# The last layer of a four-layer network: softplus in thirds, and another order of its side work

## The chip, the cores and the metric

The kernel runs on one core of a Trainium2 chip. The metric is the device time of one launch in microseconds (us), the median of several runs. The core has five engines, each with its own queue of instructions that it takes in order: TensorE (PE; PEld is its loading of weights), VectorE (DVE), ScalarE (ACT), GpSimd (POOL) and SyncE (SP), which here issues DMA transfers. Matmul results go to PSUM, which has eight banks of 512 fp32 columns on 128 partitions; SBUF is the large on-chip memory.

## The reference: what is computed

Four layers act on x of shape (2, 192, 96, 96), each as x + f(groupnorm(x)). Layers 0 to 2 (a deformable convolution, a Laplacian with a 1x1 convolution, a WKV scan) are not touched. Layer 3 is a state-space layer over the L = 9216 positions of an image, with 384 inner channels (three groups of 128) and 16 states per channel:

```
xz = x_flat @ W_in.T;  x_in, z_gate = split(xz)
x_conv = silu(depthwise_conv4(x_in) + conv_b)
dt, B_ssm, C_ssm = split(W_x @ x_conv)
delta = softplus(W_dt @ dt + 2 * b_dt)
h = exp(delta * A) * h + (delta * x_conv) * B_ssm      # along the positions
y = (sum over states of h * C_ssm) + D * x_conv
out = W_out @ (y * silu(z_gate))
```

Softplus is computed as relu(t) + ln(1 + exp(-|t|)), with a correction for what is lost in rounding when 1 is added: ln(w) - ((w - 1) - e), where e = exp(-|t|) and w = 1 + e as rounded.

## The kernel before

**Steps and units.** `layer3` cuts each image into pieces of 511 positions and two of about half that (265 and 264): 38 steps, 34 of them full. The recurrence of a step is done in 12 units, numbered q = 0 to 11 (three channel groups by four): a unit has 128 partitions that hold 16 states of 8 channels, and four rows r of them. In the loop at the end, k counts units over all steps, s is the step and q the unit in it.

**A unit.** `steps_of(k)` (L2356) spreads delta over the partitions with one matmul per row into one of five PSUM banks (`decays`, taken in turn); `decay(k)` (L2370) makes the exponentials in place on ScalarE; `times_b(k)` (L2346) multiplies the loaded delta * x_conv, `bu`, by B on POOL; `scan(k)` (L2379) is the recurrence on VectorE, four instructions; `times_c(k)` (L2403) multiplies three rows by C on VectorE into `hc`, and `times_c_aside(k)` (L2414) the fourth on POOL into `hp`; `sum_of(k)` (L2421, L2427) adds over the states on TensorE into one bank, `acc`, which lasts four units, and `gate(k)` (L2440) multiplies a finished `acc` by the gate into `y` on VectorE. `load(k)` (L2336) fetches `bu` from DRAM, and `keep(k)` (L2386) and a copy in `load` (L2340) carry the state on.

**The order.** Within unit k the engines get: `sum_of(k-2)`, `scan(k)`, `steps_of(k+1)`, `decay(k+1)`, `times_c(k)`, `gate(k-2)` where a group ends (q = 1, 5, 9), `times_c_aside(k-1)`, `times_b(k+2)`, `load(k+3)`, `keep(k)`. It is written out by hand and kept as written on TensorE, ScalarE, VectorE and POOL (`manual_schedule`); SyncE's queue is ordered by the planner.

**The side work.** Three generators run between the units, a piece up to the next `yield` at each `go(name)`:
- `early(s + 2)`: normalises x (xt to xn, L2223, L2227), then six projections (L2242) with their copies to `xi` and `zs`, three groups of convolution matmuls (L2262) with their eviction to `us`, and two Silu (L2268, L2269). 20 pieces.
- `late(s + 1)`: x_dbl (L2278), its copy and three small transfers, three matmuls for delta (L2303) with Abs and Relu (L2307, L2308), Exp and 1 + e over all three groups (L2310, L2311), the correction on VectorE (L2313) and Ln (L2314), and three POOL operations (L2316, L2318, L2320), the last followed by four stores to DRAM (`ud`, L2322) from which `load` reads. 13 pieces.
- `output(s - 1)`: the load of `xr`, two times three matmuls (L2452), each half followed by an addition on VectorE (L2460), and the store. 4 pieces.

All matmuls of the side work share one PSUM bank, `pe` (the pool `ps` has one buffer of each name). Dictionaries `AHEAD` and `BEHIND` and lines in the loop say which unit runs which pieces: those in `AHEAD` go before `sum_of`, those in `BEHIND` one before and one after `decay` (for "out" only the one before).

The pools that matter: `s1` has one buffer of each tile, `sb` two, `s3` three, `sc` four.

Of the kernel before, what the change touches and what calls it, by code (L numbers as in the profile page):

```python
# [6 lines left out]
F32 = mybir.dt.float32  # L7
I32 = mybir.dt.int32
AF = mybir.ActivationFunctionType
ALU = mybir.AluOpType  # L10
# [8 lines left out]
P = 128  # L19
CH = 96  # L20
# [43 lines left out]
class Net:  # L64
# [2021 lines left out]
    def layer3(self, x, out, stats):  # L2086
# [3 lines left out]
        nc, tc, ins = self.nc, self.tc, self.ins  # L2090
        TM = 511
# [8 lines left out]
        with ExitStack() as ctx:  # L2100
            wp = ctx.enter_context(tc.tile_pool(name="w3", bufs=1))
            s1 = ctx.enter_context(tc.tile_pool(name="l3s", bufs=1))
            sb = ctx.enter_context(tc.tile_pool(name="l3", bufs=2))
            s3 = ctx.enter_context(tc.tile_pool(name="l3h", bufs=3))
# [19 lines left out]
            b2 = self.load("b_dt", [P, ND], pool=wp)  # L2124
# [94 lines left out]
            def early(s):  # L2219

                b, t0, T = steps[s]
                xt = sb.tile([CH, 2, TM], F32, name="xt")[:, :, :T]
                nc.sync.dma_start(out=xt, in_=halves(x[b])[:, :, t0 : t0 + T])  # L2223
                xn = s1.tile([CH, 2, TM], F32, name="xn")[:, :, :T]
                gs, gb = gns[b]
                for k in range(2):
                    nc.scalar.activation(  # L2227
                        xn[:, k], xt[:, k], AF.Identity, bias=gb[:, k : k + 1], scale=gs[:, k : k + 1]
                    )
                us = s3.tile([P, ND, TM], F32, name="us")[:, :, :T]  # L2230
                zs = s3.tile([P, ND, TM], F32, name="zs")[:, :, :T]
                xi = s1.tile([P, ND, TM + 3], F32, name="xi")[:, :, : T + 3]
                got[s] = {"us": us, "zs": zs}
                if t0 == 0:
                    nc.gpsimd.memset(tail, 0.0)
                nc.scalar.copy(xi[:, :, 0:3], tail)
                yield

                def project(at):
                    pe = bank(T)  # L2240
                    for k in range(2):
                        nc.tensor.matmul(  # L2242
                            pe, w_in[:, k, at : at + P], xn[:, k], start=k == 0, stop=k == 1
                        )
                    return pe

                for d in range(ND):
                    pe = project(d * P)
                    yield
                    nc.scalar.copy(xi[:, d, 3:], pe)  # L2250
                    if d == ND - 1:
                        nc.scalar.copy(tail, xi[:, :, T : T + 3])
                    yield
                for d in range(ND):
                    pe = project(DI + d * P)
                    yield
                    nc.scalar.copy(zs[:, d], pe)
                    yield
                for d in range(ND):
                    pe = bank(T)  # L2260
                    for j in range(4):
                        nc.tensor.matmul(  # L2262
                            pe, taps[:, d, j], xi[:, d, j : j + T], start=j == 0, stop=j == 3
                        )
                    yield
                    nc.scalar.activation(us[:, d], pe, AF.Identity, bias=cb[:, d : d + 1])
                    yield
                nc.scalar.activation(zs, zs, AF.Silu)  # L2268
                nc.scalar.activation(us, us, AF.Silu)  # L2269
                yield  # L2270

            def late(s):
                us = got[s]["us"]
                T = steps[s][2]
                xd = sb.tile([NBC + DTR, TM], F32, name="xd")[:, :T]
                pe = bank(T)
                for d in range(ND):
                    nc.tensor.matmul(  # L2278
                        pe[: NBC + DTR], wx[:, d], us[:, d], start=d == 0, stop=d == ND - 1
                    )  # L2280
                yield
                nc.scalar.copy(xd, pe[: NBC + DTR])
                br = dr.tile([NBC * TM], F32, name="br")[: NBC * T].rearrange("(n t) -> n t", t=T)
                nc.sync.dma_start(out=br, in_=xd[:NBC])
                rows = []
                for name, at in (("cs", 0), ("bs", NST)):
                    t = sb.tile([P, TM], F32, name=name)[:, :T]
                    one = br[at : at + NST]
                    nc.sync.dma_start(
                        out=t,  # L2290
                        in_=bass.AP(one.tensor, one.offset, [[T, NST], [0, 8], [1, T]]),
                    )
                    rows.append(t)
                dl = sb.tile([P, ND, TM], F32, name="dl")[:, :, :T]
                du = s1.tile([P, ND, TM], F32, name="du")[:, :, :T]
                ud = dr.tile([ND * P * TM], F32, name="ud")[: ND * P * T]
                ud = ud.rearrange("(i v e r t) -> i v e r t", i=ND, v=NV, e=8, r=4)
                got[s].update(xd=xd, cs=rows[0], bs=rows[1], dl=dl, ud=ud)
                ln = s1.tile([P, ND, TM], F32, name="ln")[:, :, :T]
                yield  # L2300
                for d in range(ND):
                    pe = bank(T)
                    nc.tensor.matmul(  # L2303
                        pe, wdt[:, d * P : (d + 1) * P], xd, start=True, stop=True
                    )
                    yield
                    nc.scalar.activation(du[:, d], pe, AF.Abs, bias=b2[:, d : d + 1])  # L2307
                    nc.scalar.activation(dl[:, d], pe, AF.Relu, bias=b2[:, d : d + 1])  # L2308
                    yield
                nc.scalar.activation(du, du, AF.Exp, scale=-1.0)  # L2310
                nc.scalar.activation(ln, du, AF.Identity, bias=1.0)  # L2311
                yield
                nc.vector.scalar_tensor_tensor(du, ln, -1.0, du, ALU.add, ALU.subtract)  # L2313
                nc.scalar.activation(ln, ln, AF.Ln)  # L2314
                yield
                nc.gpsimd.tensor_tensor(ln, ln, du, ALU.subtract)  # L2316
                yield
                nc.gpsimd.tensor_tensor(dl, dl, ln, ALU.add)  # L2318
                yield
                nc.gpsimd.tensor_tensor(du, dl, us, ALU.mult)  # L2320
                for r in range(4):
                    nc.sync.dma_start(  # L2322
                        out=ud[:, :, :, r].rearrange("i v e t -> (v e) i t"),
                        in_=du[32 * r : 32 * r + 32],
                    )
                yield
# [72 lines left out]
            def times_c(k):  # L2399
                s, q, _, _ = where(k)  # L2400
                T = steps[s][2]
                hc = sb.tile([P, 3, TM], F32, name="hc")[:, :, :T]
                nc.vector.tensor_tensor(  # L2403
                    hc,
                    got[s]["h", q][:, :3, 1:],
                    got[s]["cc"].unsqueeze(1).to_broadcast([P, 3, T]),
                    ALU.mult,
                )
                got[s]["hc", q] = hc
# [62 lines left out]
            for k in range(2):  # L2472
# [1 line left out]
            rows_c(0)  # L2474
            steps_of(0)
            decay(0)
            AHEAD = {1: "late", 7: "early", 8: "early", 9: "early"}
            BEHIND = {
                0: "late",
                1: "late",  # L2480
                2: "late",
                3: "out",
                4: "out",
                5: "early",
                6: "early",
                7: "early",
                8: "early",
                9: "early",
                10: "early",
            }  # L2490
            running = {"out": iter(()), "late": iter(()), "early": iter(())}

            def go(name):
                next(running[name], None)

            for k in range(nk):
# [5 lines left out]
                if q == 3 and s + 2 < ns:  # L2502
                    running["early"] = early(s + 2)
                if q in AHEAD:
                    go(AHEAD[q])
                    go(AHEAD[q])
                if k >= 2:
                    sum_of(k - 2)
                if q == 0 and s:
                    rows_c(s)  # L2510
                scan(k)
                if q in (4, 5):
                    go("out")
                if k + 1 < nk:
                    steps_of(k + 1)
# [4 lines left out]
                if q in BEHIND and BEHIND[q] != "out":  # L2520
                    go(BEHIND[q])
                if q == 3:
                    go("late")
                    go("early")
                times_c(k)
                if k >= 2 and (k - 2) % NV == NV - 1:
                    gate(k - 2)
                if q == 4:
                    go("late")
                if q == 11:  # L2530
                    go("early")
                if k:
                    times_c_aside(k - 1)
                if k + 2 < nk:
                    times_b(k + 2)
                if q in (5, 6, 7):
                    go("late")
                if k + 3 < nk:
                    load(k + 3)
# [100 lines left out]
```

## Time and profile before

| | us |
|---|---|
| median of 3 runs | 10381.23 (10363.35 to 10385.16) |
| the profiled execution | 10366.8 |
| its span (first to last instruction) | 10365.0 |
| VectorE busy | 8345.7 (81%) |
| TensorE busy | 9044.9 (87%) |
| POOL busy | 6997.7 (68%) |
| ScalarE busy | 6080.6 (59%) |
| 7550 to 10050 us, in layer 3: VectorE, TensorE, POOL, ScalarE busy, of 2500 | 2332.47, 2250.93, 2228.77, 1548.58 |
| the same: granted TensorE clock | 0.90 |

The profile is of one execution. A row of a timeline gives the start, the duration, the engine, the line, the operation, `output<-input` with shapes, and in brackets the idle time of the engine before it with what ended it. Where a row stands for several instructions (x4), the duration is that of all of them. A row of waits gives the total, the number of times and the longest. The granted clock is the share of full speed that TensorE's throttle allowed. Matmul ends are modelled.

### The profile page before, as it was taken

The numbers are of one execution on the slowest core, as the hardware profiler recorded it, in microseconds if no ns is written. First come the engines' busy times: TensorE is split into PE (matmuls) and PEld (weight loads), VectorE is DVE, ScalarE is ACT, GpSimd is POOL, SyncE is SP. The second block draws the span as 40 slices with busy tenths as digits, with TensorE's granted clock in tenths as the row PEclk, the third lists the DMA queues.
The fourth block names the chain that finished last, engine by engine and source line by source line (L and its number), as shares of the span: only waits on it lengthen the run. The fifth ranks groups of instructions, "written<-read, shape, count | busy, mean of one in ns | idle before, by whom it ended". The sixth has DMA issues, their size and how long they took to land. (4 is left out here: it accounts for less than half of the span.)

```text
span 10365.0 us, 222647 instructions
## 1 busy us (share of the span) xinstructions
PE 9044.9 (87%) x87686; PEld 5317.9 (51%) x87686; DVE 8345.7 (81%) x8842; ACT 6080.6 (59%) x11850; POOL 6997.7 (68%) x5645
## 2 busy tenths in 40 slices
PE   4799999999889999999776677887889989898988
PEld 3588788788767888888622222223222222222223
DVE  5788888788677777777655789884999999999999
ACT  0366666666566777777500178664666666666665
POOL 1466666766566666666501268773888998888898
PEclk8899999999999999999888798887888998989988
DMA  8455555555434555555444344434777777777776
GB/s 148 92 140 135 136 138 136 136 135 139 112 95 131 136 136 138 136 139 138 112 125 130 125 149 154 128 110 95 171 169 172 175 173 171 172 172 169 172 168 149
DMA packets 877166, 1465.19 MB, mean 141 GB/s; under 512 B 251616, under 2 KB 682276, under 8 KB 875012
## 3 DMA queue, kind: packets, MB, share of 16 engines
q1 hardware_dynamic: 663276, 1264.09, 48.7%
q0 software_dynamic: 104000, 133.19, 5.7%
q10 hardware_dynamic: 108840, 53.57, 2.1%
q8 instruction: 701, 11.49, 0.5%
q14 instruction: 349, 2.86, 0.1%
HBM read 871.06 MB, written 381.46 MB: 121 GB/s over the span
## 5 line engine op out<-in xcount | busy, mean ns | idle before, releaser
L581 DVE TENSOR_TENSOR sp<-h 128x2304 f32<-128x2304 f32 x790 | 2160.6, 2767 | 41.9 <-ACT h L560 41.9
L2346 POOL TENSOR_TENSOR bu<-bu,bs 128x2044 f32<-128x2044 f32 (+2 forms) x456 | 1970.8, 4322 | 230.9 <-DMA bu<-ud 181.8
L2379 DVE TENSOR_TENSOR_SCAN h<-da,bu 128x512 f32<-128x512 f32 (+2 forms) x1824 | 1979.8, 1146 | 102.6 <-ACT da L2370 86.3
L605 ACT COPY st<-pt 128x512 f32<-128x512 f32 (+1 forms) x2370 | 1213.5, 515 | 1094.0 <-PE pt L597 1022.7
L597 PE MATMUL pt<-ident,sp 128*128 128x128 f32 x14220 | 1677.4, 276 | 82.0 <-DVE sp L581 38.9
L603 DVE COPY st<-pt 128x512 f32<-128x512 f32 x1580 | 1062.7, 687 | 817.7 <-PE pt L597 806.0
L597 PEld LDWEIGHTS pt<-ident,sp 128*128 128x128 f32 x14220 | 1567.6, 142 | 164.6 <-issue 96.9
L551 POOL TENSOR_TENSOR h<-u,step 128x1152 f32<-128x1152 f32 (+1 forms) x474 | 1100.6, 2340 | 672.3 <-DVE u L524 479.2
L569 POOL DMA_DIRECT2D xw<-xp_d x2500 | 1389.8, 622 | 189.0 <-PE pt L648 83.7
L2370 ACT ACTIVATE da<-da,nA 128x511 f32<-128x511 f32 (+2 forms) x1824 | 1065.0, 638 | 575.1 <-PE da L2356 567.9
L648 PE MATMUL pt<-st,xw 64*32 64x288 f32 (+1 forms) x30000 | 1095.1, 370 | 144.2 <-DVE st L603 62.1
L674 ACT COPY val<-pt 128x288 f32<-128x288 f32 (+1 forms) x3000 | 957.6, 404 | 286.7 <-PE pt L648 262.4
L2356 PE MATMUL da<-dl,spread 32*128 32x511 f32 (+2 forms) x3648 | 927.3, 659 | 117.7 <-DVE h L2379 117.6
L776 PE MATMUL pf<-main,wd 126*64 126x128 f32 (+1 forms) x17064 | 985.4, 274 | 9.7 <-DMA far_m<-val 9.2
L776 PEld LDWEIGHTS pf<-main,wd 126*64 126x64 f32 x17064 | 912.9, 140 | 155.8 <-issue 150.9
L2403 DVE TENSOR_TENSOR hc<-h,cc 128x1533 f32<-128x1533 f32 (+2 forms) x456 | 755.1, 1656 | 171.3 <-PE acc L2427 169.3
L648 PEld LDWEIGHTS pt<-st,xw 64*32 64x32 f32 x30000 | 546.4, 106 | 558.4 <-ACT val L674 170.1
L797 PE MATMUL pf<-more,wl 118*64 118x144 f32 (+5 forms) x11592 | 732.7, 277 | 2.3 <-DMA more<-far_l 2.0
L797 PEld LDWEIGHTS pf<-more,wl 118*64 118x64 f32 (+1 forms) x11592 | 665.0, 137 | 69.6 <-issue 63.2
L2356 PEld LDWEIGHTS da<-dl,spread 32*128 32x128 f32 x3648 | 297.9, 195 | 708.3 <-DVE h L2379 491.0
L2414 POOL TENSOR_TENSOR hp<-h,cs 128x511 f32<-128x511 f32 (+2 forms) x456 | 555.4, 1218 | 68.4 <-DVE h L2379 39.1
L2242 PE MATMUL pe<-xn,sb_w_in 96*128 96x511 f32 (+2 forms) x912 | 507.6, 686 | 91.3 <-ACT xi L2250 41.5
(344 smaller groups left out, 13105.0 us busy)
## 6 DMA issues: line engine op xcount, KB each, us to landing
bu<-ud SPq DMA_DIRECT2D x408, 1022.0 KB
main<-val SPq DMA_DIRECT2D x2016, 91.1 KB
far_l<-val SPq DMA_DIRECT2D x288, 324.0 KB
xw<-xp_d POOLq DMA_DIRECT2D x2500, 26.0 KB
far_m<-val SPq DMA_DIRECT2D x288, 162.0 KB
half_d<-hv SPq DMA_DIRECT2D x54, 768.0 KB
hv<-half_d SPq DMA_DIRECT2D x54, 768.0 KB
more<-far_l SPq DMA_DIRECT2D x576, 60.8 KB
```

The costliest lines, as they stand in the source:

```text
L551: nc.gpsimd.tensor_tensor(hs, u[:, :, 8 * KK * l : 8 * KK * l + n].unsqueeze(3).to_broadcast([P, 2, n, WS]), con["step"].unsqueeze(1).unsq ...
L569: nc.gpsimd.dma_start(out=xw[e * WN : (e + 1) * WN, i], in_=xp_d[y : y + WS, x : x + WS, e * CM // 2 : e * CM // 2 + XW],)
L581: nc.vector.tensor_tensor(sp.rearrange("p s (y x) -> p s y x", x=WS), hy.unsqueeze(3).to_broadcast([P, n, WS, WS]), hx.unsqueeze(2).to_bro ...
L597: nc.tensor.transpose(pt[:, q], sp[:, 2 * (q0 + q) : 2 * (q0 + q) + 2].rearrange("p e w -> p (e w)"), self.ident,)
L605: nc.scalar.copy(st[:, q0 : q0 + m], pt[:, :m])
L648: nc.tensor.matmul(to, xw[e * WN : (e + 1) * WN, win, g * CG : g * CG + 32], sts[pair][e * WN : (e + 1) * WN].rearrange("p s (r c) -> p s ...
L776: nc.tensor.matmul(place(cv, m, 2 - t // 3, 2 - t % 3, None, 0), con["wd"][:, cv, t, m * CO : (m + 1) * CO], blocks(took, 1, rows), start= ...
L797: nc.tensor.matmul(place(cv, m, 2 * cv if alone else 1 - cv, 2 - t, h, 1 - alone,), con["wl"][lanes, slot, t, m * CO : (m + 1) * CO], bloc ...
L2346: nc.gpsimd.tensor_tensor(bu, bu, got[s]["bs"].unsqueeze(1).to_broadcast([P, 4, steps[s][2]]), ALU.mult)
L2356: nc.tensor.matmul(das[r][:, 1:], spread[at, v].rearrange("p n e -> p (n e)"), got[s]["dl"][at, i], start=True, stop=True, tile_position=( ...
L2370: nc.scalar.activation(da, da, AF.Exp, scale=nA[:, 4 * q + r : 4 * q + r + 1])
L2379: nc.vector.tensor_tensor_scan(h[:, r], got[s]["da", q][r], bu[:, r], 0.0, ALU.mult, ALU.add)
```

## The change

It touches `layer3` alone.

- In `late`, each third of softplus is finished by itself: Relu, then Abs in place in the `pe` bank, Exp in place there, 1 + e into `ln`, and the correction on VectorE with one operand from that bank. Before, Abs went to SBUF, and Exp, 1 + e and the correction ran over all three thirds. `late` has 15 pieces now, and Ln comes by itself after the last correction.
- `late` runs in q = 0 to 3 behind (one piece before and one after `decay`), with one more piece after `times_c` in q = 1, 2, 3 (the correction of the third) and Ln in q = 3; the POOL operations go in q = 4, 5, 6 instead of 5, 6, 7.
- `output`'s matmuls go in q = 4 and 5 instead of 3 and 4, its additions in 5 and 6 instead of 4 and 5.
- `early`'s pieces go in q = 6 to 11 instead of 5 to 11 (its first in q = 3 as before); q = 10 gets four.
- `hc` has three buffers instead of two, and `xt` one instead of two.

```diff
-                xt = sb.tile([CH, 2, TM], F32, name="xt")[:, :, :T]
+                xt = s1.tile([CH, 2, TM], F32, name="xt")[:, :, :T]
...
-                    nc.scalar.activation(du[:, d], pe, AF.Abs, bias=b2[:, d : d + 1])
                     nc.scalar.activation(dl[:, d], pe, AF.Relu, bias=b2[:, d : d + 1])
+                    nc.scalar.activation(pe, pe, AF.Abs, bias=b2[:, d : d + 1])
+                    nc.scalar.activation(pe, pe, AF.Exp, scale=-1.0)
+                    nc.scalar.activation(ln[:, d], pe, AF.Identity, bias=1.0)
                     yield
-                nc.scalar.activation(du, du, AF.Exp, scale=-1.0)
-                nc.scalar.activation(ln, du, AF.Identity, bias=1.0)
-                yield
-                nc.vector.scalar_tensor_tensor(du, ln, -1.0, du, ALU.add, ALU.subtract)
+                    nc.vector.scalar_tensor_tensor(
+                        du[:, d], ln[:, d], -1.0, pe, ALU.add, ALU.subtract
+                    )
+                    yield
                 nc.scalar.activation(ln, ln, AF.Ln)
                 yield
...
-                hc = sb.tile([P, 3, TM], F32, name="hc")[:, :, :T]
+                hc = s3.tile([P, 3, TM], F32, name="hc")[:, :, :T]
...
-            AHEAD = {1: "late", 7: "early", 8: "early", 9: "early"}
-            BEHIND = {0: "late", 1: "late", 2: "late", 3: "out", 4: "out",
-                5: "early", 6: "early", 7: "early", 8: "early", 9: "early", 10: "early"}
+            AHEAD = (7, 8, 9, 10)
+            BEHIND = {4: "out", 5: "out"}
+            BEHIND.update({q: "late" for q in range(4)})
+            BEHIND.update({q: "early" for q in range(6, 11)})
...
                 scan(k)
-                if q in (4, 5):
+                if q in (5, 6):
                     go("out")
...
                 if q == 3:
-                    go("late")
                     go("early")
                 times_c(k)
+                if q in (1, 2, 3):
+                    go("late")
+                if q == 3:
+                    go("late")
                 if k >= 2 and (k - 2) % NV == NV - 1:
                     gate(k - 2)
-                if q == 4:
-                    go("late")
...
-                if q in (5, 6, 7):
+                if q in (4, 5, 6):
                     go("late")
```

In the changed kernel the correction is L2312, and the lines behind it move by two: `scan` is L2381, `times_c` L2405, `gate` L2442 and the additions of `output` L2462.

More of the change, by code (lines that the diff above doesn't have):

```diff
@@ L2476, in layer3 @@
             decay(0)
-            AHEAD = {1: "late", 7: "early", 8: "early", 9: "early"}
[L2478 to L2490, printed above, removed]
+            AHEAD = (7, 8, 9, 10)
+            BEHIND = {4: "out", 5: "out"}
+            BEHIND.update({q: "late" for q in range(4)})
+            BEHIND.update({q: "early" for q in range(6, 11)})
             running = {"out": iter(()), "late": iter(()), "early": iter(())}
@@ L2504, in layer3 @@
                 if q in AHEAD:
-                    go(AHEAD[q])
-                    go(AHEAD[q])
+                    go("early")
+                    go("early")
                 if k >= 2:
```

## The prediction

> **What bounds the kernel now.** I read the waits, then one step of layer 3 instruction by instruction, then the chain of waits there. A step is 511 positions and has 12 units, q = 0 to 11; S(q) is the time at which the unit's first scan starts. Only layer 3 changes, and its loop has 34 full steps and 4 of half the length, which I count as 36.
>
> Waits of VectorE from 7000 to 10200 us (total, times, longest):
>
> ```profile
> DVE hc L2403 <- PE acc L2427: 165.9, 147, 3.8
> DVE h L2379 <- ACT da L2370: 84.7, 46, 32.0
> DVE h L2379 <- POOL bu L2346: 9.4, 5, 3.6
> ```
>
> VectorE hardly waits: its work is the bound, with 166 us of waits for a free hc buffer on top. One step, from q1 on, in VectorE's own order:
>
> ```profile
> 8590.89 4.57 DVE L2379 TENSOR_TENSOR_SCAN h<-da,bu 128x512 f32<-128x512 f32 x4 [1.38 <-ACT da L2370]
> 8595.90 1.75 DVE L2403 TENSOR_TENSOR hc<-h,cc 128x1533 f32<-128x1533 f32 x1 [0.45 <-PE acc L2427]
> 8597.57 0.68 DVE L2440 TENSOR_TENSOR y<-acc,zs 128x511 f32<-128x511 f32 x1
> 8598.17 4.55 DVE L2379 TENSOR_TENSOR_SCAN h<-da,bu 128x512 f32<-128x512 f32 x4
> 8602.64 1.72 DVE L2403 TENSOR_TENSOR hc<-h,cc 128x1533 f32<-128x1533 f32 x1
> 8604.29 4.56 DVE L2379 TENSOR_TENSOR_SCAN h<-da,bu 128x512 f32<-128x512 f32 x4
> ...
> 8610.41 4.55 DVE L2379 TENSOR_TENSOR_SCAN h<-da,bu 128x512 f32<-128x512 f32 x4
> 8614.88 0.66 DVE L2460 TENSOR_TENSOR xr<-pe,xr 96x511 f32<-96x511 f32 x1
> 8615.46 1.74 DVE L2403 TENSOR_TENSOR hc<-h,cc 128x1533 f32<-128x1533 f32 x1
> 8617.12 5.39 DVE L2313 SCALAR_TENSOR_TENSOR du<-ln,du 128x1533 f32<-128x1533 f32 x1
> 8622.43 4.55 DVE L2379 TENSOR_TENSOR_SCAN h<-da,bu 128x512 f32<-128x512 f32 x4
> ```
>
> A unit with nothing else is 6.12 (8598.17 to 8604.29): scans 4.47, hc 1.65. From the starts of L2313 at 7647.26 and 9769.97, 24 steps apart, a step is **88.45**. The scan starts give the units: q1 7.28, q2 6.12, q3 6.12, q4 12.02 (with L2313), q5 7.32, q6 6.33, q7 7.01, q8 7.02, q9 9.21, q10 6.12, q11 6.12, q0 7.57; sum 88.2.
>
> How soon a unit's decays follow, from TensorE and ScalarE (unit q3 starts at 8604.29):
>
> ```profile
> 8604.76 4.14 PE L2356 MATMUL da<-dl,spread 32*128 32x511 f32 x8
> 8608.83 4.51 PE L2452 MATMUL pe<-y,sb_w_out 128*96 128x511 f32 x6
> ...
> 8608.94 0.66 ACT L2370 ACTIVATE da<-da,nA 128x511 f32<-128x511 f32 x1 [0.45 <-PE da L2356]
> ```
>
> There are five decay banks, so the fourth matmul of `steps_of(k+1)` waits for the third scan of unit k. TensorE is free at S+4.54, the fourth exponential starts at S+4.65. Whatever TensorE gets behind `steps_of` starts no sooner.
>
> **Removed.** L2313 leaves q4: 5.3 us (mean 5.37). It takes 1.75 at 8091.20 and otherwise ends some 1.6 after the POOL product beside it; hc, with one operand in PSUM, keeps to 1.72 beside POOL. Three new ones of 511 elements read PSUM too: nearest row y (acc in PSUM, zs in SBUF), 0.60 from start to next start, together 1.8. Lower end a third of 1.75 (0.58), upper end a third of 5.37 (1.8 each). So **-3.5** in VectorE's work.
>
> The hc waits: in the step shown 0.45 at q1, 0.66 at q7 and q8, 2.37 at q9. Three buffers remove the wait as such, but TensorE's order is unchanged: the same matmuls that made `sum_of` late stand before `steps_of`, so the next scan waits for its decay instead.
>
> **Added: the wait for the thirds.** At q1, q2, q3 VectorE's queue is scan, hc, then the new L2312, which needs ScalarE's last operation of the third. Count from S: TensorE is free at 4.55; the wdt matmul takes 1.15 to ScalarE's start (8593.74 to 8594.89), so 5.70; Relu 0.59, Abs 0.68, Exp 0.68 and Identity 0.69, with 0.04 before each that waits for the one before, as between L2310 (ends 8522.06) and L2311 (starts 8522.10): 2.72. Ready at 8.45, seen at 8.5. VectorE is there at 6.12. **The stall is 2.35, three times.** Queued behind it: the gate at q1 and the next scans, hence decays, POOL's hp, everything. So q1 = 6.12 + 2.35 + 0.6 + 0.6 (gate) = 9.7; q2 = q3 = 9.1. In q1 nothing else is later: wx ends at S(q1)+2.2.
>
> ScalarE's longer work (0.7 x 6 for two of 1.48, about +1.2 a step) lies in that chain. Ln now waits for L2312 at the end of q3: xn 1.45, table load 1.28, Ln 1.4, copies 0.2, table load 1.28, first decay 0.66 make S(q4)+5.9, just before VectorE wants it at 6.12. So q4 = 6.1; were the two table loads or xn longer by 0.3, the excess would be a wait.
>
> **Output matmuls.** First half now behind `steps_of` in q4, second in q5 behind the residual addition. The gate of q5 writes y, of which there is one tile, so it must wait for that second half; before, a whole unit lay between. First half from S(q4)+4.66, 4.5 long (8608.83), ends S(q5)+3.0; sum 1.0, steps 1.1; the addition ends at S(q5)+5.05; second half 2.75 (as at 8615.60): 7.9. The gate could go at 6.7 (4.47 + 0.58 + 1.65). q5 = 8.55; q6 takes the other addition, 6.7. The xr load and output store go a unit later with them; the next xr is a step away.
>
> **Early, now in q6 to q10.** One pe bank: each matmul waits for the eviction before it. The first projection starts in q6 after the addition (S(q6)+5.1), a unit later than before, and the whole must still end with q10, so q8 to q10 get four pieces each. Rows for this part:
>
> ```profile
> 8561.02 1.99 PE L2242 MATMUL pe<-xn,sb_w_in 96*128 96x511 f32 x4
> 8564.07 3.70 PE L2262 MATMUL pe<-xi,taps 128*128 128x511 f32 x8 [1.06 <-ACT zs L2257]
> 8573.29 1.02 PE L2421 MATMUL acc<-us,skip 128*128 128x511 f32 x2
> ```
>
> q7: two projections 2.0 each, sum 1.0, steps 1.1, all in time: 6.1. q8: the copy of the last projection stands behind the decays, so the next begins at S+2.1; 1.95 + 1.0 + 1.1 + decay 0.75: 6.9. q9: a projection ahead instead of a taps group: 7.05 by the same sum, where before had 9.21. **q10** is where it is paid: the first taps group, behind q9's `steps_of` (S(q9)+6.25), ends 3.65 later, at S(q10)+2.85; its eviction takes 0.65; the second group stands ahead of `sum_of` and `steps_of`: 3.5 + 3.65 + skip and sum 1.95 + steps 1.1 + decay 0.75 = **11.0**, against 6.12. q11 6.1 and q0 7.6 stay (Silu with its table loads).
>
> Sum: 9.7 + 9.1 + 9.1 + 6.1 + 8.55 + 6.7 + 6.1 + 6.9 + 7.05 + 11.0 + 6.1 + 7.6 = 94.0, **+5.6 a step** at full clock.
>
> **Cold TensorE.** The clock granted is 0.50 in 8535.9 to 8540.1, after 4.41 us without matmuls, and 0.61 in 8519.9 to 8524.3, after paced decay matmuls only. In the first stretch the fourth decay matmul comes 2.13 after its scan instead of 1.2, and a projection takes twice its time. The stalls leave TensorE idle 4 us between q1 and q2 (the skip matmul waits for the gate) and some 2.6 in q3. Cost: 0 to 0.9 in q2; 0 to 1.7 in q3 (0.9 and 0.8 for wdt); 0 to 1.5 in q5; together 0 to 4.1. I take 1.3, since the clock is back within a few us of dense matmuls (1.00 at 8547). The Trainium skill, "TensorE: Matmul & The Clock Gate", Part 1, has the clock halved after about 3.4 us without activity; by that only the first gap would count, some 0.9, while the rows show 0.61 without such a gap.
>
> **At nothing.** POOL's three operations (3.42 each) a unit sooner: POOL waits 171.6 us for bu's transfers and 91.0 for Ln, which mostly goes, but scans waited 9.4 us for POOL in all, so at most that is gained; ud's four stores and the bu loads behind them in SP's queue only come sooner. One tile of x: its load waits for xn of the step before, and SP issues it right behind that, a step ahead; bu loads behind it wait for later scans anyway. Exposed, 383.2 KB at 171 GB/s would be 2.2 a step, 80 us.
>
> So 5.6 + 1.3 = 6.9 a step, x 36 = +248. The profiled execution took 10366.8 (span 10365.0), 0.14% under the median: **10615**. Its own range, 5.6 to 9.7 a step, is 10568 to 10716.
>
> **Rivals.** (1) Faster: VectorE's saved work is kept, because TensorE runs ahead in q6 to q10 and is ready for the output before the gate. Then the regrouping costs nothing, all hc waits (4.1) and 5.3 go, 1.8 and the three stalls come: 88.45 - 9.4 + 1.8 + 3 x 2.35 = 87.9, x 36 is -20, 10347; with stalls half as long, -3.5 more a step, 10220. It decides at a stall of 2.5. For it: VectorE is busiest (93% in 7550 to 10050). Against: the single pe bank. Chance 0.10, of which some falls within 0.2%. (2) The stalls are as computed, but q10's wait is hidden (taps evicted sooner): 5.6 - 4.9 + 1.3 = +2, 10440, and half hidden 10530. Chance 0.14. (3) The change doesn't bite: hc and thirds cancel, within 0.2%: 0.05. (4) TensorE cold all through q6 to q10 too: a taps group in q10 costs 3.65 more, 13.35 a step in all, 10847. For it: 0.50 on a projection at 8540; against: 1.00 on all of them after 8547. Chance 0.09. The forecast has 0.62.
>
> Range 10440 to 10740: it leaves out (1), (3) and the upper half of (4). What this kernel's measurement can tell from no change is about 0.2%, 21 us. Faster 0.08, same 0.07, slower 0.85.
>
> **What would show it.** Right: a VectorE wait of 2.3 to 4 before L2312, on ScalarE, three a step; L2312 near 0.68; hc without waits; a gate waiting for TensorE once a step; about 5 us before the scan of q11, on da; L2313's 5.3 gone; a step of 94 to 98. Wrong: L2312 without idle time before it, or q10's scan in time, or L2312 above 1 us.

## The result, and the profile after

The changed kernel takes 10766.81 us (median, 10762.33 to 10773.55); the kernel before, run beside it, 10372.29 (10358.21 to 10385.16). The ratio is **1.0381, 95% interval 1.0363 to 1.0399**: 394.5 us slower. The forecast had the sign and the places, but not the size: 10615, and the range ended at 10740. The profiled execution has a span of 10765.2, 400.2 over that of before.

Waits of VectorE in the kernel after, from 7000 to 10600 us (total us, times, longest):

```profile
DVE du L2312 <- ACT ln L2310: 418.9, 111, 36.4
DVE h L2381 <- ACT da L2372: 255.1, 110, 36.2
DVE y L2442 <- PE pe L2454: 79.7, 33, 2.5
DVE h L2381 <- POOL bu L2348: 56.0, 35, 5.5
```

The longest of the first and of the second line (36.4 and 36.2) stand once, ahead of the loop, where the kernel before has 41.6 and 32.0. The wait for an hc buffer (165.9 before) is gone, and so is L2313; in their place stand the wait before the corrections, a longer one for the decays, the gate's wait for the output matmuls, and some for POOL. VectorE, 93% busy before, is busy for 80%: 1919 of 2400 us in 7550 to 9950.

One step of it in VectorE's own order, from q1 on:

```profile
8885.93 4.57 DVE L2381 TENSOR_TENSOR_SCAN h<-da,bu 128x512 f32<-128x512 f32 x4 [1.41 <-ACT da L2372]
...
8894.75 0.69 DVE L2312 SCALAR_TENSOR_TENSOR du<-ln,pe 128x511 f32<-128x511 f32 x1 [2.61 <-ACT ln L2310]
...
8895.95 4.56 DVE L2381 TENSOR_TENSOR_SCAN h<-da,bu 128x512 f32<-128x512 f32 x4
...
8906.01 0.69 DVE L2312 SCALAR_TENSOR_TENSOR du<-ln,pe 128x511 f32<-128x511 f32 x1 [3.85 <-ACT ln L2310]
8906.61 4.56 DVE L2381 TENSOR_TENSOR_SCAN h<-da,bu 128x512 f32<-128x512 f32 x4
...
8916.79 0.69 DVE L2312 SCALAR_TENSOR_TENSOR du<-ln,pe 128x511 f32<-128x511 f32 x1 [3.97 <-ACT ln L2310]
...
8932.83 0.69 DVE L2442 TENSOR_TENSOR y<-acc,zs 128x511 f32<-128x511 f32 x1 [2.46 <-PE pe L2454]
...
8971.18 4.57 DVE L2381 TENSOR_TENSOR_SCAN h<-da,bu 128x512 f32<-128x512 f32 x4 [4.46 <-ACT da L2372]
```

The number in brackets is idle time. Three stalls before the corrections, one before the gate of q5, one before the first scan of q11. From 8885.93 to the same place of the next step (8984.92) it is 98.99 us. By the starts of the scans:

| unit | q1 | q2 | q3 | q4 | q5 | q6 | q7 | q8 | q9 | q10 | q11 | q0 | sum |
|---|---|---|---|---|---|---|---|---|---|---|---|---|---|
| before | 7.28 | 6.12 | 6.12 | 12.02 | 7.32 | 6.33 | 7.01 | 7.02 | 9.21 | 6.12 | 6.12 | 7.57 | 88.2 |
| forecast at full clock | 9.7 | 9.1 | 9.1 | 6.1 | 8.55 | 6.7 | 6.1 | 6.9 | 7.05 | 11.0 | 6.1 | 7.6 | 94.0 |
| after | 10.02 | 10.66 | 10.78 | 6.12 | 9.92 | 6.72 | 6.11 | 6.88 | 7.37 | 10.67 | 6.13 | 7.61 | 99.0 |

The 34 full steps take 3358.5 us (7290.92 to 10649.40) where they took 3004.0 (7258.02 to 10261.98): +354.5, 10.4 each. The four half steps and the end take 42.5 more (29.7 for the two ahead of the full ones, 12.8 for the two behind and the end), the pieces ahead of the loop 3.2. That is the whole 400.

### The profile page after: what moved, and what is told of

Read it like the earlier page. It is cut to its first block, busy times and chain, and to the rows that moved or that the text cites. A ratio compares the mean times of both kernels' runs of the same rounds, so it can differ in the third digit from the quotient of the medians.

```text
span 10765.2 us, 223017 instructions
## 1 busy us (share of the span) xinstructions
PE 9221.1 (86%) x87686; PEld 5361.4 (50%) x87686; DVE 8225.5 (76%) x8918; ACT 6099.1 (57%) x12002; POOL 6985.0 (65%) x5645
## 4 chain that ended last, share of the span: by engine, by line
PE 28%; ACT 10%; DVE 10%; issue 2%; POOL 1%; DMA 0%; SPq 0%; DVEq 0%; ACTq 0%; POOLq 0%
PE da L2358 6%; ACT da L2372 4%; PE pe L2262 4%; PE acc L2429 3%; PE pe L2242 3%; PE pe L2454 3%; DVE h L2381 2%; PE pe L1523 2%; DVE opq L1882 2%; PE pe L2278 1%; PE pe L1515 1%; PE acc L2423 1%; PE v L1732 1%; PE pm L1997 1%; PE pe L2303 1%
## 5 line engine op out<-in xcount | busy, mean ns | idle before, releaser
L2381 DVE TENSOR_TENSOR_SCAN h<-da,bu 128x512 f32<-128x512 f32 (+2 forms) x1824 | 1980.9, 1148 | 319.1 <-ACT da L2372 260.1
L2358 PE MATMUL da<-dl,spread 32*128 32x511 f32 (+2 forms) x3648 | 1034.3, 701 | 162.7 <-DVE h L2381 160.9
L2358 PEld LDWEIGHTS da<-dl,spread 32*128 32x128 f32 x3648 | 344.5, 210 | 855.4 <-issue 432.4
L2405 DVE TENSOR_TENSOR hc<-h,cc 128x1533 f32<-128x1533 f32 (+2 forms) x456 | 751.3, 1648 | 0.0
L2242 PE MATMUL pe<-xn,sb_w_in 96*128 96x511 f32 (+2 forms) x912 | 451.8, 620 | 130.1 <-ACT xi L2250 65.2
```

The costliest lines, as they stand in the source:

```text
L2358: nc.tensor.matmul(das[r][:, 1:], spread[at, v].rearrange("p n e -> p (n e)"), got[s]["dl"][at, i], start=True, stop=True, tile_position=( ...
L2381: nc.vector.tensor_tensor_scan(h[:, r], got[s]["da", q][r], bu[:, r], 0.0, ALU.mult, ALU.add)
```

## The experiments

Theory A: the loss is VectorE's idle time before the corrections, lengthened by TensorE's slow clock, and besides it the gate's wait for y and, in q10, the group of convolution matmuls (a taps group) that stands ahead of `sum_of`. Theory B: the one `pe` bank and TensorE's order set the step in any case, and the idle times only show it. Ratios are to the kernel before, run on the same chip; the kernel after stands at 1.0381. Profiles are of one execution of each.

### Two parts alone, and two of the suspected causes taken away

**e1_defer**: the corrections a unit later, behind the scans of the next unit.

```diff
                 scan(k)
+                if q in (2, 3, 4):
+                    go("late")
...
                 times_c(k)
-                if q in (1, 2, 3):
-                    go("late")
-                if q == 3:
+                if q == 4:
                     go("late")
...
-                if q in (4, 5, 6):
+                if q in (5, 6, 7):
                     go("late")
```

> The kernel after, with each correction (L2312) one unit later: VectorE takes it behind the four scans of the next unit instead of behind hc of its own unit, the last one in q4; Ln and POOL's three operations move a unit later with it, as in the kernel before. Theory A (the loss of a step is VectorE standing idle before the corrections, 2.6 + 3.85 + 3.97 us in the step read, TensorE's slow clock included): all of that goes, the units q1 to q4 become 6.7 each, a step about 87, x 36 about -430: 10330. Theory B (TensorE and ScalarE with the one pe bank set the step anyway, VectorE's idle time only shows it): the idle time turns up again before the scans of q3 to q6, the step stays above 95, over 10620.

Measured: 10429.48, ratio 1.0054 (1.0038 to 1.0069): 337 us less than the kernel after. VectorE in q2 of e1_defer and at the start of q3, then in q8:

```profile
8894.26 4.56 DVE L2381 TENSOR_TENSOR_SCAN h<-da,bu 128x512 f32<-128x512 f32 x4
8898.74 0.66 DVE L2312 SCALAR_TENSOR_TENSOR du<-ln,pe 128x511 f32<-128x511 f32 x1
...
8900.97 4.56 DVE L2381 TENSOR_TENSOR_SCAN h<-da,bu 128x512 f32<-128x512 f32 x4
...
8938.64 4.57 DVE L2381 TENSOR_TENSOR_SCAN h<-da,bu 128x512 f32<-128x512 f32 x4 [2.68 <-ACT da L2372]
```

The stalls are gone, and units of 6.7 stand where 10.7 stood (8894.26 to 8900.97). Theory A is right in the main; this step is 89.9 (8894.26 to 8984.16), 3 above the forecast, because a wait of 2.7 for the decays turns up in q8. Two projections ahead of it and the stretch of the second show why:

```profile
8928.24 2.90 PE L2242 MATMUL pe<-xn,sb_w_in 96*128 96x511 f32 x4 [0.57 <-DVE xr L2462]
8931.81 3.77 PE L2242 MATMUL pe<-xn,sb_w_in 96*128 96x511 f32 x4 [0.68 <-ACT xi L2250]
```

They take 2.90 and 3.77 instead of 1.98, and the granted clock is 0.50 in 8930 to 8934, where in q7 and q8 of the kernel after it was 1.00 (8940 to 8953). That much is theory B's.

**e2_hc3**: the kernel before with three buffers of hc and one of xt.

```diff
-                xt = sb.tile([CH, 2, TM], F32, name="xt")[:, :, :T]
+                xt = s1.tile([CH, 2, TM], F32, name="xt")[:, :, :T]
-                hc = sb.tile([P, 3, TM], F32, name="hc")[:, :, :T]
+                hc = s3.tile([P, 3, TM], F32, name="hc")[:, :, :T]
```

> The kernel before, with nothing changed but three buffers of hc and one of xt. Theory A (the wait for a free hc buffer is only moved to the next scan, which waits for its decay, because TensorE's order is the same): the wait hc<-acc is gone, about 4 us a step of it comes back as the scan's wait for da and the gate's for acc; gain 0 to 1 us a step, 10340 to 10372. Theory B (the waits were a loss of their own): all 4 us a step gained, about 10220.

Measured: 10371.17, ratio 0.9993 (0.9984 to 1.0002): no difference. VectorE's waits in e2_hc3:

```profile
DVE h L2379 <- ACT da L2370: 231.9, 230, 32.0
DVE y L2440 <- PE acc L2427: 36.6, 37, 3.0
```

These are from 7100 to 10600, where the kernel before waits 169.3 for an hc buffer and 86.3 for decays. Of the hc waits none is left; the scans wait 231.9 for their decays, and the gate 36.6 for acc. The wait has moved. The single tile of x was not run by itself; the two together bring and cost nothing.

**e7_hc2**: the kernel after with two buffers of hc (`hc = sb.tile(`), the same question from the other side.

> The kernel after with two buffers of hc instead of three, nothing else. Theory A (the wait for hc and the wait of the next scan for its decay are the same delay of TensorE): hc waits for acc in q8 to q10, the scans behind it no longer wait for da; 10767 within 20. Theory B (the third buffer is what keeps the changed order from being worse): over 10850.

Measured: 10766.9, ratio 1.0373 (1.0355 to 1.0390): the time of the kernel after. hc waits 139.1 us in 7300 to 10260, the scans for their decays 38.8 instead of 166.9.

**e3_warm**: the kernel after with three matmuls more, that nobody reads, in each of q1, q2 and q3.

```diff
+            def fill(k):
+                s = where(k)[0]
+                T = steps[s][2]
+                for _ in range(3):
+                    nc.tensor.matmul(
+                        decays[(4 * k + 8) % 5][:, 1 : T + 1],
+                        skip[:, 0],
+                        got[s]["us"][:, 0],
+                        start=True,
+                        stop=True,
+                    )
...
                 if q in BEHIND:
                     go(BEHIND[q])
+                if q in (1, 2, 3) and s + 1 < ns:
+                    fill(k)
```

> The kernel after, with three more full matmuls (128 x 128 on 511 columns) behind the delta matmul in q1, q2 and q3, into the decay bank that is free there and is overwritten later; their results are used by nobody. They fill TensorE's idle time and nothing waits for them. Theory A (q2, q3 and q5 are 1.6, 1.7 and 1.4 us longer than worked out at full clock because the granted clock is 0.50 there): the clock stays near 1.00 in q2 to q4, the idle time before the corrections falls to 2.4 to 2.6 in all three, a step is about 94, x 36 about -180: 10590. Theory B (ScalarE's four operations and not the clock made those units longer): unchanged, 10767, or slower by what the matmuls take.

Measured: 10684.55, ratio 1.0312 (1.0291 to 1.0334): adding work takes 82 us off. The four times lie further apart than elsewhere (10647.40 to 10731.13), and the profile is of the shortest, 120 under that of the kernel after. The stretches q1, q2, q3 and q5 of a step, in the kernel after and then in e3_warm (length; busy us of PE, PEld, DVE, ACT, POOL; granted clock; DMA share; GB/s):

```profile
8885.93:8895.95 10.02, 5.68 (x22) 1.36 (x20) 7.41 (x7) 7.30 (x16) 10.02 (x4) 0.84 0.65 167
8895.95:8906.61 10.66, 8.16 (x30) 1.82 (x30) 6.80 (x7) 5.36 (x11) 6.60 (x3) 0.80 0.67 156
8906.61:8917.39 10.78, 9.41 (x18) 2.69 (x18) 6.81 (x7) 5.14 (x10) 5.72 (x2) 0.52 0.42 97
...
8923.51:8933.43 9.92, 9.28 (x28) 2.50 (x26) 7.46 (x8) 4.21 (x11) 9.92 (x4) 0.80 0.80 196
```

```profile
8916.58:8928.14 11.56, 9.34 (x28) 2.26 (x26) 7.41 (x7) 7.30 (x16) 11.56 (x5) 0.84 0.75 172
8928.14:8937.02 8.88, 8.71 (x24) 2.94 (x25) 6.80 (x7) 4.99 (x10) 5.45 (x3) 0.83 0.45 116
8937.02:8945.91 8.89, 8.87 (x32) 2.76 (x33) 6.81 (x7) 5.43 (x10) 5.74 (x3) 0.98 0.50 112
...
8952.03:8960.68 8.65, 7.88 (x27) 2.02 (x25) 7.40 (x8) 4.22 (x11) 8.65 (x4) 0.86 0.78 186
```

In q3 the clock goes from 0.52 to 0.98, in q4 (left out above) from 0.50 to 0.92. q2, q3 and q5 fall from 10.66, 10.78 and 9.92 to 8.88, 8.89 and 8.65: to within 0.25 of what I had worked out at full clock. The mean clock of q2 hardly moves (0.80 and 0.83); what moves is where it is low. Its skip matmul, and the delta matmul of q3, which took 2.07 each in the kernel after, now run at full speed:

```profile
8928.28 1.12 PE L2423 MATMUL acc<-us,skip 128*128 128x511 f32 x2 [2.36 <-DVE y L2442]
...
8941.64 1.12 PE L2303 MATMUL pe<-xd,wdt 44*128 44x511 f32 x2
```

ScalarE's four operations are unchanged. So the clock is the missing part, 4.9 us in these three units. Not all of it shows in the time, 3.3 a step in the profiled execution and 2.3 by the medians: q1 rises by 1.5 (the clock is now 0.50 in 8916 to 8920, at its start), and the scans wait 99.7 for POOL's bu in place of 56.0.

**e4_whole**: the kernel after with softplus over all three thirds as before; `late`'s pieces are those of before, with Exp and 1 + e in q3, the correction and Ln in q4, POOL in q5 to q7. What is left of the change is the regrouping, with the three hc buffers and the one tile of x.

> The kernel after, with softplus again over all three thirds as in the kernel before (Abs to SBUF, Exp, 1 + e, and one correction of 1536 columns behind hc of q4, Ln and POOL's operations in q5 to q7): the regrouping, three hc buffers and one xt alone. Theory A: no idle time in q1 to q3 (units 6.1 to 6.7), the correction of 5.3 back in q4, the gate's wait in q5 and the decay's wait of 4.5 before the scan of q11 stay: a step about 93, 10530, slower than the kernel before by 1.5 per cent. Theory B (the regrouping is harmless without the thirds, since TensorE runs ahead): 10370 or less.

Measured: 10610.8, ratio 1.0210 (1.0186 to 1.0233). The regrouping alone costs 237 us; the thirds, in their own unit, cost another 156 on top, and a unit later (e1_defer) they gain 181. The scans wait 434.4 us for their decays in 182 places (4.33, 0.81, 0.21, 4.81 and 1.41 in one step, before the scans of q8 to q11 and q1), the gate 112.0 for the output matmuls. My 10530 counted the waits in q5 and q10 but not the one of 2.7 to 4.3 before the scan of q8, where the slow clock had moved to (0.50 in 8600 to 8604, ahead of the scan of q8 at 8607.61).

### The parts of the regrouping

**e5_y2**: two buffers of y (`got[s]["y"] = sb.tile(`), and two of hc.

> The kernel after with two buffers of y, and hc in two again (there is no room for both). Theory A (in q5 VectorE's gate stands still until the second half of the output matmuls has read the only y): that wait, 79.7 us in all, goes, the scans of q6 and all behind them come 2.2 us sooner; the hc buffer taken back costs nothing, since what waited for it waits for its decay anyway; 10685. Theory B (the same TensorE work is in the way either way): the time comes back as a wait of the scans of q6 to q8 for their decays, 10767. If the hc buffer were worth its 4 us a step, 10830.

Measured: 10745.7, ratio 1.0357 (1.0340 to 1.0374); 21 us less, and its interval overlaps that of the kernel after. The gate's wait is gone altogether, and most of it is given back in two places: before the corrections 347.6 us in 7300 to 10260 (315.7 in the kernel after; the one of q1 is 3.83 instead of 2.61), before POOL's bu 94.2 (46.6). Neither theory had this. In the first 5 us of the q1 read the clock is 0.69 (8965 to 8970), where it is 0.94 in the kernel after (8885.93 to 8891): with the stall gone, there is a slow stretch here as well. Why POOL is later was not run.

**e6_taps**: the last two taps groups behind `steps_of` of q10 and q11.

```diff
-            AHEAD = (7, 8, 9, 10)
+            AHEAD = (7, 8, 9)
-            BEHIND.update({q: "early" for q in range(6, 11)})
+            BEHIND.update({q: "early" for q in range(6, 12)})
```

> The kernel after with the last two groups of convolution matmuls moved: the second behind steps_of in q10 (instead of ahead of sum_of), the third behind steps_of in q11. Theory A (the second group ahead of sum_of and steps_of is what makes the scan of q11 wait 4.5 us for its decay): that wait goes; the Silu comes later and makes the scan of q1 wait some 1.6 longer; 3 us a step less, 10660. Theory B (TensorE has that much work there in any order): the wait turns up in q0 and q1 in full, 10767.

Measured: 10711.62, ratio 1.0321 (1.0304 to 1.0339): 55 us less. The wait before the scan of q11 is gone, and the one before q1 is 3.31 instead of 1.41, as worked out; the size is half of it.

**e9_pool_later**: the kernel after with POOL's three operations in q5, q6, q7.

> The kernel after with POOL's three operations in q5, q6 and q7, as in the kernel before; the four stores to ud go a unit later with them. My prediction put their move at nothing: 10767 within 20. Rival: being sooner, POOL's product and the stores that wait for it stand in SP's queue ahead of loads of bu that could go, so POOL waits 224 us for transfers where it waited 172 before, and scans wait 56 for POOL where they waited 9; putting the three back a unit gains up to 1.3 us a step, 10720; or, if the stores are then late for the loads of the next step, it costs.

Measured: 10765.35, ratio 1.0372 (1.0354 to 1.0390): nothing. The rival was right on the mechanism: scans wait 10.2 us for POOL's bu instead of 56.0. But the scans then wait for their decays, 205.6 instead of 166.9 in 7300 to 10260: where POOL was late, TensorE was as late.

### A version that beats both

**e7_defer_y2**: e1_defer with two buffers of y and two of hc.

> The kernel after with each correction a unit later (as in e1_defer), y in two buffers and hc in two. e1_defer took 10429 with 1.25 to 2.8 us of wait for y in its q5; if that wait adds to the rest, 60 us less: 10370, level with the kernel before. If TensorE's chain through the pe bank sets q5 to q11, no change: 10429.

Measured: 10295.42, ratio 0.9930 (0.9910 to 0.9950): 134 less than e1_defer, more than twice the 60 worked out. The 2.7 of q8 went with the wait for y; in the step read, q5 to q10 wait only 0.51, 0.66 and 4.20, all for acc.

**e8_defer_y2_taps**: with the taps groups of e6_taps too.

> e7_defer_y2 with the convolution matmuls moved as in e6_taps. If the three losses (corrections in their own unit, the wait for y, the group ahead of sum_of in q10) are separate and add, a step is about 85.5, 10270, faster than both the kernel before and the kernel after. If the pe bank's chain binds in any order, 10370 to 10429.

Measured: 10268.58, ratio 0.9896 (0.9880 to 0.9913). It beats both kernels, and the time is the one worked out for three separate losses. The parts are not: the taps groups brought 55 in e6_taps and 27 here, the wait for y 21 in e5_y2 and 134 in e7_defer_y2. So that the sum fits is in part luck. Scans now wait 69.1 us for POOL's bu.

**e10_pool_first**: and POOL's second and third operation ahead of `hp` and `times_b` in q6 and q7.

```diff
+                if q in (6, 7):
+                    go("late")
                 if k:
                     times_c_aside(k - 1)
                 if k + 2 < nk:
                     times_b(k + 2)
-                if q in (5, 6, 7):
+                if q == 5:
                     go("late")
```

> e8_defer_y2_taps with POOL's second and third operation of late ahead of hp and times_b in q6 and q7 instead of behind them, so that the stores to ud are issued some 5.8 us sooner and the loads of bu behind them in SP's queue too. e8_defer_y2_taps took 10269 with 69 us of scans waiting for POOL's bu. If SP's queue is behind that: 40 to 70 us less, 10200 to 10230. If POOL's own work is (times_b then comes 3.4 later): 10269 or more.

Measured: **10198.28, ratio 0.9830 (0.9814 to 0.9846)**. VectorE's waits over 7300 to 10260 us and SP's wait for POOL's product over 7000 to 10600, in e10_pool_first:

```profile
DVE h L2381 <- ACT da L2372: 106.5, 37, 3.3
...
DVE h L2381 <- POOL bu L2348: 4.7, 4, 2.1
```

```profile
SPq L2324 <- POOL du L2322: 254.2, 38, 13.9
```

SP waits 254.2 for the product (446.7 in e8_defer_y2_taps), POOL waits 36.8 for bu's transfers (148.5, both in 7300 to 10260), and scans wait 4.7 for POOL's bu (69.1). What is left is in the main the wait of 3.3 a step for the decays in front of q1, which stand behind the Silu.

## Why the prediction was wrong in size and right in its places

- **The stalls before the corrections** stand where they were put, three a step, on ScalarE. Worked out: 2.35 each; measured: 2.61, 3.85, 3.97. L2312 takes 0.69, 0.60 from start to next start, as taken. In q1 the delta matmul is in time, but Relu stands behind the four exponentials in ScalarE's queue and starts at S + 6.29 (8892.22) instead of 5.70; the chain counted TensorE's queue only.
- **The step that failed is "Cold TensorE"**: 1.3 us a step of 0 to 4.1. Measured: 4.6 in the three units it names (1.56 in q2, 1.68 in q3, 1.37 in q5), of 5.0 that the step is over the sum (99.0 less 94.0). It was taken low because the clock had come back "within a few us of dense matmuls". In the kernel after it did so once, in q2, and was lost again in the stall that follows; q3 and q4 have mostly decay matmuls paced by the scans:

```profile
8895.95:8899.00 3.05, 2.91 (x10) 0.70 (x10) 3.05 (x4) 0.00 (x0) 0.87 (x1) 0.50 0.93 207
8899.00:8906.61 7.61, 5.26 (x28) 1.12 (x20) 3.75 (x4) 5.36 (x11) 5.73 (x2) 0.92 0.56 136
8906.61:8926.00 19.39, 17.37 (x28) 5.42 (x29) 15.42 (x15) 12.82 (x22) 10.61 (x5) 0.51 0.43 106
```

The last number but two is the clock: 0.50, 0.92, then 0.51 for 19 us. TensorE and ScalarE in q2 and q3 of the kernel after show how that reaches the corrections:

```profile
8896.09 2.07 PE L2423 MATMUL acc<-us,skip 128*128 128x511 f32 x2 [4.49 <-DVE y L2442]
...
8907.98 4.27 PE L2358 MATMUL da<-dl,spread 32*128 32x511 f32 x6 [3.72 <-DVE h L2381]
8912.17 2.07 PE L2303 MATMUL pe<-xd,wdt 44*128 44x511 f32 x2
```

```profile
8901.19 2.39 ACT L2372 ACTIVATE da<-da,nA 128x511 f32<-128x511 f32 x4 [6.30 <-PE da L2358]
8903.48 0.70 ACT L2307 ACTIVATE dl<-pe,sb_b_dt 128x511 f32<-128x511 f32 x1
...
8912.28 0.66 ACT L2372 ACTIVATE da<-da,nA 128x511 f32<-128x511 f32 x1 [0.46 <-PE da L2358]
8914.28 0.69 ACT L2307 ACTIVATE dl<-pe,sb_b_dt 128x511 f32<-128x511 f32 x1 [1.34 <-PE pe L2303]
```

In q3 the fourth decay comes 1.0 late (8912.28 is S + 5.67, worked out 4.65) and the delta matmul takes 2.07, not 1.12. In q2 something I had no term for comes on top: the skip matmul (2.07 where 1.12 was the price) delays `steps_of` as a whole, so all four exponentials run in one burst of 2.3, and Relu stands behind them in ScalarE's queue, at S + 7.5 instead of 5.7. The bound of 0.9 for q2 was therefore too low. e3_warm shows both to be the clock's doing: with the skip and the delta matmul at 1.12, the stalls of q2 and q3 are 2.08 each.
- **The halves were mis-sized.** I counted a half step as half. The two ahead of the full steps lost 14.9 each, more than a full one's 10.4; the four and the end lost 42.5, where 13.8 was counted. Why a half step loses that much was not run. With 6.9 for 10.4 in each of 34 full steps (120 us short), and 3.2 ahead of the loop, this makes up the difference of 152.
- **L2313's 5.3 went**, q4 is 6.12, and Ln with its table loads was in time.
- **The gate's wait for y**: there, 2.46 instead of 1.2; the first half of the output matmuls started at S(q4) + 5.56 instead of 4.66 and took 5.03 instead of 4.5, at the slow clock.
- **q10**: 10.67 for 11.0; q8 and q11 to 0.03. q9 is 0.32 over and q10 0.33 under; that they cancel is luck. And e5_y2 and e6_taps show that such a term is not what its removal brings: 21 and 55 us came of 82 and 107.
- **hc's third buffer**: right that the wait only moves (e2_hc3, e7_hc2).
- **POOL at nothing**: right in the time, by e9_pool_later, though wrong in saying that POOL's waits would mostly go: it waits 224.3 for transfers (171.6 before) and 145.9 ahead of L2318 (91.0 before). With the operations a unit later (e9_pool_later) the transfers' part is 181.9, and SP waits 352.5 for POOL's product instead of 478.5, which fits the four stores that wait for it having held up loads behind them in SP's queue.
- **Rivals.** That TensorE is cold all through (10847) came nearer in number than the forecast, but by luck: q6 to q10, where it put the cost, ran at full clock. The faster rival was wrong on its own deciding point, a stall of 2.5, and on the regrouping, which costs 237 by itself (e4_whole).

What stays open: how the clock's drops follow from a step's length. In e1_defer, e3_warm, e4_whole and e5_y2 they moved to another unit or stood there as well, and no run here tells beforehand in which.

## What to carry to other kernels

Where a queue taken in order gets an operation that needs a chain of three engines, add up the chain from the thing that starts it in that unit and compare it with the work ahead of it in the queue; if it is longer, put the operation one unit later (here 337 us of the 394). Count every queue on the way, the chain's own engines' too. A wait for a buffer may be worth nothing (169 us here); look at what the next instruction waits for. Where a change gives TensorE idle time, take its slow rate (2.07 for 1.12 here) as the upper end in every unit that holds little but paced matmuls.

## What the hardware showed that was not expected

- In the kernel after TensorE's clock was 0.50 in 8895.95 to 8899 and 0.50 to 0.55 from 8906.61 to 8926, although the idle times ahead of its rows there were no longer than 4.5, 3.7 and 0.7 us and the rows call it busy most of the time (17.37 of 19.39): decay matmuls of 32 rows that are paced by the scans did not keep the clock up. Three full matmuls a unit mostly did (0.98 in q3 of e3_warm, but 0.70 in 8932 to 8937, in its q2).
- The correction of 1533 columns with both operands in SBUF and POOL's product take turns, as these rows of the kernel before show:

```profile
8090.87 6.45 POOL L2346 TENSOR_TENSOR bu<-bu,bs 128x2044 f32<-128x2044 f32 x1 [0.42 <-ACT da L2370]
8091.20 1.75 DVE L2313 SCALAR_TENSOR_TENSOR du<-ln,du 128x1533 f32<-128x1533 f32 x1
```

In five of the 34 full steps L2313 took 1.75, and beside it the product took 6.45 to 6.67; all other products took 4.48 to 4.57, and L2313 mostly 5.3 to 6.9. With one operand in PSUM it was 0.69 per third beside POOL.
- Exp and 1 + e out of the PSUM bank took 0.58 and 0.60 for 511 columns; Relu and Abs with a bias 0.70 and 0.69.
